# Filtered up and down sampling on half-array tiles, with the middle rows in passes of their own and one pinned order

## The chip, the cores and the metric

The kernel runs on one core of one Trainium2 chip. The metric is the device time in microseconds. The kernel before takes 1045.09 us, the median of three runs (1044.65, 1045.09 and 1049.59).

## The reference

The input `x` has the shape (4, 32, 128, 128): 4 batches, 32 tokens (channels) of 128 rows and 128 columns, in float32. Two layers follow each other, each a mixer and a recurrence, and each is added to its input:

```python
x = x + L0_conv(_ln_c(x), ...)          # attention over tokens with spectral convolutions
t = _to_tokens(x)                       # here 4 x 4096 x 128: tokens and rows in one axis
t = t + L0_ffn(_ln_t(t), W, V, ...)     # recurrence
x = _from_tokens(t, x)
x = x + L1_conv(_ln_c(x), bias, up_filter, dn_filter)
t = t + L1_ffn(_ln_t(t), W, V, ...)
```

`_ln_c` and `_ln_t` normalise each row of 128 numbers by its mean and variance. The recurrence multiplies the rows by W, normalises the products over all rows (batch norm), and then steps along the rows: `y = sigmoid(wx + y @ V.T)`.

The change is in the second layer's mixer, `L1_conv`:

```python
x = x + bias
x = x.reshape(B * C, 1, H, W)                       # 128 images of 128 x 128
x = jnp.repeat(jnp.repeat(x, 2, axis=2), 2, axis=3) # 256 x 256
x = _conv_same(x, up_filter)                        # 12 x 12, outer product of one 1-D filter
x = jax.nn.leaky_relu(x, negative_slope=0.2) * sqrt(2)
x = _conv_same(x, dn_filter)                        # 12 x 12, the same
x = x[:, :, ::2, ::2]                               # back to 128 x 128
```

Both filters are outer products, so each convolution is a product along the rows' axis and one along the columns' axis. Doubling and filtering along one axis is one matrix of 128 by 256, filtering and halving is one of 256 by 128. These matrices are banded: an output depends on a handful of neighbouring inputs only, since the filter has 12 taps at double resolution.

## The kernel before

The residual stays on the chip in `XA`, a tile of 128 partitions (the row h) by 4 batches, 32 tokens and 128 columns. `WXY` is one large tile that holds the recurrences' products and states; its last columns, `rest`, hold the convolution's matrices and starting states.

The function `parallel()` sets the stages. The first layer's mixer takes the time up to about 487 us; its instructions' order is written out by hand and pinned by `in_order()` (L433), which makes each instruction of PE, VectorE (DVE), ScalarE (ACT) and GpSimd (POOL) depend on the one before it on its engine. The first recurrence's scan (`scan()`, steps on L1846 to L1848) runs from 487 to about 548 us, in four segments side by side. Then comes the convolution stage (to about 961 us), then the second scan, which also adds the states to the residual and writes the output.

The convolution stage works on units of half a token, that is two images of 128 by 128; there are 64 units. Each unit passes through four functions:

- `up_rows` (L1976 to L1982): two products, each with an image of `XN` (128x128) as the stationary operand and the matrix `UR` of 256 columns as the moving one. The result lies transposed in PSUM. ACT copies its 512 columns to `q1` (L1981).
- `up_cols` (L1984 to L1993): for each half s of the 256 output positions, one product with `UC[s]` stationary and `q1` moving (512 columns); then leaky relu, as a relu on ACT (L1991) and a multiply and add on DVE (L1992), into `U`.
- `down_cols` (L1995 to L2004): eight products with a 128x128 piece of `U` stationary and `DC[s]` moving, two of them summed into each result; ACT copies to `q3` (L2003).
- `down_rows` (L2006 to L2012): two products with `DR[r]` stationary and 256 columns of `q3` moving, summed; DVE adds the result to `XA` (L2012).

Beside the units runs work on whole tokens or groups of up to four tokens. A table `beside` says at which step each is issued:

- `with_states`: the first recurrence's states of a token are turned (PE, L1900) and added to `XA` (DVE, L1931), and the rows' statistics are taken (L317).
- `input_norm`: scales and offsets of a group of tokens from these statistics. This is a chain of small DVE operations (L307 to L312), the addition of epsilon (DVE, L291), the power -1/2 (POOL, L292), the offset (DVE, L325) and the channel's bias (DVE, L1939).
- `input_images`: the scaled images `XN`, half of them on DVE (L1948), half on ACT (L1950).
- `complete`: statistics of the finished token and its store to DRAM (`turned`).
- `feature_norm`, `feature_rows`, `feature_columns`, `feature_products`: the norm, scaled rows (DVE L356, ACT L358), turned rows (PE L364, ACT L372) and products with W (PE L378, statistics on DVE L381, copy on ACT L385) for the second recurrence.

At step k the loop issues `down_rows(k-4)`, `down_cols(k-3)`, `up_cols(k-1)`, `up_rows(k)`, and then what `beside` lists. The stage isn't pinned: a scheduler orders the instructions by their dependencies. Groups are of 1, 1, 2 and then 4 tokens. `U` and `XN` have three buffers (pool `cv3`), the other tiles of the stage two. In PSUM, `ps_c1` has one buffer for each of five tags; turned rows use the two buffers of `ps_t`.

The eight filter matrices come by one DMA (L1907) ahead of the first scan.

## Time and profile before

| | us |
|---|---|
| median of three runs | 1045.09 |
| span of the profiled execution | 1043.7 |
| first scan's first product to its last (L1846) | 487.4 to 547.3 |
| convolution stage at its steady pace | 564 to 940 |
| last statistics of the second recurrence's products (L381) | 960.4 |
| mean granted TensorE clock over the span | 0.955 |

Busy time by stretch, in us:

| stretch | PE | DVE | ACT | POOL | granted clock |
|---|---|---|---|---|---|
| 0 to 360 (loads, mixer) | 305.8 | 271.5 | 224.5 | 69.1 | |
| 360 to 547.6 (mixer's end, first scan) | 164.6 | 166.8 | 158.6 | 55.1 | 0.99 |
| 547.6 to 564 (stage's start) | 12.2 | 13.8 | 4.7 | 2.0 | 0.69 |
| 564 to 940 (stage) | 370.6 | 235.8 | 211.0 | 43.9 | 1.00 |
| 940 to 961 (stage's end) | 17.4 | 13.6 | 14.0 | 2.0 | 1.00 |
| 961 to 1043.7 (second scan) | 69.2 | 72.3 | 52.5 | 0.6 | 0.90 |

PE, PEld, DVE, ACT, POOL and SP stand for TensorE's products, TensorE's weight loads, VectorE, ScalarE, GpSimd and SyncE. A group line of the profile gives the line of the code, the engine, the operation, the tiles (out<-in), for TensorE the tile of the array in use (128*128 is the whole of it, 64*128 is 64 rows by 128 columns), the shapes, and how many there were. The numbers after the bar are the busy time of the group in us, the mean of one in ns, and the idle time of the engine just before them with what ended most of it. A line of the timeline gives the start in us from the span's start and the length of a run of like instructions. A line of the stretches gives the busy time of each engine between two times, the granted clock, the share of the DMA engines and GB/s.

### The profile page before, as it was taken

The page shows a single profiled execution, that of the slowest core. Times are in us where ns is not written, and L with a number is a line of the kernel's source. Part 1 is how long each engine was busy: PE and PEld are TensorE (multiplying, and loading weights), DVE is VectorE, ACT ScalarE, POOL GpSimd, SP SyncE. Part 2 cuts the span into 40 slices and gives each one's busy share as a digit, 9 for nine tenths or more (in the row PEclk, how much of TensorE's full clock was granted, in tenths as well). Part 3 has the DMA queues.
Part 4 walks back from the last instruction along what each step waited for, and adds up shares of the span by engine and source line. Part 5 has one row for each costly group of instructions (what it writes and reads, how often), then busy time and mean ns, then how long its engine had stood idle before and what let it go on. Part 6 is the DMA issues. An engine that isn't in the chain of part 4 may idle for free.

```text
span 1043.7 us, 18129 instructions
## 1 busy us (share of the span) xinstructions
PE 939.8 (90%) x6422; PEld 679.4 (65%) x6422; DVE 773.7 (74%) x2501; ACT 665.3 (64%) x1606; POOL 172.8 (17%) x298
## 2 busy tenths in 40 slices
PE   3999899977888999877998999999999999998995
PEld 2565565775655555534776777777777777775884
DVE  5996487776688998988888565665666666466997
ACT  3756355766467999877883545464656555556874
POOL 1000000022444536441001111102020202100000
PEclk9999989977889999999998999999999999999998
DMA  9723000001011110200000001000000000004543
GB/s 235 175 36 76 1 1 1 1 1 42 21 42 41 42 42 22 82 21 1 1 1 1 21 21 31 21 21 21 22 21 21 21 21 28 24 21 166 212 163 131
DMA packets 68965, 48.83 MB, mean 47 GB/s; under 512 B 4417, under 2 KB 63809, under 8 KB 68801
## 3 DMA queue, kind: packets, MB, share of 16 engines
q1 hardware_dynamic: 68529, 47.31, 15.6%
q8 instruction: 53, 0.87, 0.4%
q0 software_dynamic: 288, 0.01, 0.2%
q10 hardware_dynamic: 48, 0.26, 0.1%
q14 instruction: 47, 0.39, 0.1%
HBM read 30.68 MB, written 16.88 MB: 46 GB/s over the span
## 4 chain that ended last, share of the span: by engine, by line
PE 47%; DVE 26%; ACT 8%; POOL 6%; issue 3%; POOLq 0%; DVEq 0%; ACTq 0%
PE ps_up L1989 8%; PE ps_scan L1846 7%; PE ps_dn L2001 6%; DVE XA L1516 4%; PE ps_up L1978 3%; DVE XA L1515 3%; PE ps_dn L2010 3%; PE ps_y L1235 2%; POOL c_r L292 2%; PE pm L987 2%; PE ps_wx L378 2%; DVE U L1992 2%; PE ps_inv L413 2%; DVE ps_scan L1847 2%; PE ps_st L1358 2%
## 5 line engine op out<-in xcount | busy, mean ns | idle before, releaser
L1992 DVE SCALAR_TENSOR_TENSOR U<-ps_up,above 128x512 f32<-128x512 f32 x128 | 86.7, 690 | 89.9 <-ACT above L1991 89.8
L1989 PE MATMUL ps_up<-q,WXY 128*128 128x512 f32 x256 | 124.0, 606 | 6.0 <-ACT q L1981 6.0
L2001 PEld LDWEIGHTS ps_dn<-WXY,U 128*128 128x128 f32 x1024 | 124.4, 192 | 3.3
L2001 PE MATMUL ps_dn<-WXY,U 128*128 128x128 f32 x1024 | 124.6, 275 | 0.0
L1847 DVE SCALAR_TENSOR_TENSOR ps_scan<-WXY,bs,ps_scan 128x128 f32<-128x128 f32 x352 | 101.7, 351 | 11.1 <-PE ps_scan L1846 9.7
L1991 ACT ACTIVATE above<-ps_up 128x512 f32<-128x512 f32 x128 | 74.4, 596 | 25.4 <-PE ps_up L1989 25.4
L2003 ACT COPY q<-ps_dn 128x512 f32<-128x512 f32 x64 | 37.5, 586 | 71.9 <-PE ps_dn L2001 71.9
L378 PE MATMUL ps_wx<-xt,wvt 128*128 128x512 f32 x128 | 68.0, 617 | 6.5 <-ACT WXY L385 4.5
L1978 PEld LDWEIGHTS ps_up<-WXY,XN 128*128 128x128 f32 x256 | 49.6, 194 | 34.8 <-issue 15.9
L292 POOL TENSOR_TENSOR f_r<-rs_e,neg_half 128x16 f32<-128x16 f32 (+2 forms) x10 | 24.0, 2396 | 278.4 <-DVE rs_e L291 278.4
L1989 PEld LDWEIGHTS ps_up<-q,WXY 128*128 128x128 f32 x256 | 44.0, 193 | 39.1 <-issue 23.9
L1978 PE MATMUL ps_up<-WXY,XN 128*128 128x256 f32 x256 | 67.4, 387 | 0.1
L2010 PE MATMUL ps_dn<-q,WXY 128*128 128x256 f32 x256 | 66.0, 380 | 0.0
L782 PE MATMUL ps_st<-cst,XA 128*128 128x130 f32 x256 | 43.7, 311 | 14.7 <-ACT XA L765 11.6
L2010 PEld LDWEIGHTS ps_dn<-q,WXY 128*128 128x128 f32 x256 | 46.1, 190 | 16.4 <-issue 12.0
L385 ACT COPY WXY<-ps_wx 128x512 f32<-128x512 f32 x60 | 35.0, 583 | 33.6 <-DVE bn L381 33.4
L1573 ACT ACTIVATE xn<-XA,f_o,f_r 128x128 f32<-128x128 f32 x120 | 50.9, 489 | 4.7 <-DVE f_o L1555 4.7
L782 PEld LDWEIGHTS ps_st<-cst,XA 128*128 128x128 f32 x256 | 35.4, 207 | 27.8 <-ACT XA L765 12.7
L1352 ACT ACTIVATE Z<-Z,k,aB 128x128 f32<-128x128 f32 x128 | 51.1, 481 | 3.5 <-DVE Z L1347 3.2
L1515 DVE SCALAR_TENSOR_TENSOR XA<-ps_inv,r1B,xin 128x128 f32<-128x128 f32 x128 | 44.1, 344 | 8.8 <-PE ps_inv L1508 8.8
L1516 DVE SCALAR_TENSOR_TENSOR XA<-Z,gB,XA 128x128 f32<-128x128 f32 x128 | 46.5, 363 | 5.0
L1950 ACT ACTIVATE XN<-XA,c_o,c_r 128x128 f32<-128x128 f32 x64 | 28.8, 490 | 31.5 <-DVE c_o L1939 25.5
(433 smaller groups left out, 2135.0 us busy)
## 6 DMA issues: line engine op xcount, KB each, us to landing
XA<-in_x_dram SPq DMA_DIRECT2D x16, 512.0 KB, 7.9
xin<-in_x_dram SPq DMA_DIRECT2D x32, 256.0 KB, 3.1
turned<-XA SPq DMA_DIRECT2D x32, 256.0 KB, 2.3
XA<-turned SPq DMA_DIRECT2D x8, 1024.0 KB, 14.6
out_dram<-res SPq DMA_DIRECT2D x64, 128.0 KB, 2.1
WXY<-dd SPq DMA_DIRECT2D x4, 544.0 KB, 10.6
WXY<-md SPq DMA_DIRECT2D x4, 144.0 KB, 4.9
WXY<-m1d SPq DMA_DIRECT2D x1, 544.0 KB, 10.9
```

Source lines behind the costliest of these rows:

```text
L378: mm(self.held[t], self.t[:, 0, :], xt, start=True, stop=True)
L782: mm(p[:, i, :], XA[:, b, t0 + j + i, :], cst[:, C_E : C_E + 130], start=True, stop=True)
L1515: stt(a, p2[c, b][:, i], r1B[:, j : j + 1], xin[c, b - b % 2][:, b % 2, i], ALU.mult, ALU.add)
L1516: stt(a, Z[c][:, b, i], gB[c][:, n : n + 1], a, ALU.mult, ALU.add)
L1846: mm(p4, self.t[:, 1, :], prev, start=True, stop=True)
L1847: stt(p4, WX[:, :, h, :], s[:, 0:1], p4, ALU.mult, ALU.add)
L1978: mm(p[:, b, :], XN[u // 2][:, (u % 2) * H2 + b, :], UR.rearrange("p r q -> p (r q)"), start=True, stop=True)
L1989: mm(p, UC[:, s, :], q, start=True, stop=True)
L1991: nc.scalar.activation(above, p, AF.Relu, scale=1.0 - SLOPE)
L1992: stt(U[:, s], p, SLOPE, above, ALU.mult, ALU.add)
L2001: mm(p[:, r, b, :], U[:, s, b, r * P : (r + 1) * P], DC[:, s, :], start=(s == 0), stop=(s == 1))
L2010: mm(p, DR[:, r, :], q[:, r], start=(r == 0), stop=(r == 1))
```

## The change

The banded matrices are cut, so that products run on half of the array's rows or half of its columns.

- The image's 128 rows and columns are cut into two halves of 64. `up_rows` multiplies, for each half of the image's rows, only with the 67 positions (`E`) of each phase that this half reaches, so that there are two products of 64 rows and 134 columns for each image, into two tiles `p1a` and `p1b`. Positions close to the cut need both halves.
- `up_cols` likewise has, for each of two parts and two halves, a product of 64 rows with 268 moving columns.
- Because `down_cols` for a half of the outputs needs rows beyond the cut, the middle rows get passes of their own: 16 columns around the cut of each of eight images (`XM`, copied by POOL) go through `up_rows` together as a third image in every fourth unit (so that they come out side by side on the 128 partitions), then through `mid_cols`, `mid_leaky`, `mid_down` and `mid_copy` (once for every eight images). `down_mid` (POOL) adds their contribution to the 12 middle columns of `q3`.
- `down_cols` has 16 products (32 MATMULs) for a unit, each on one half of the array's columns with 64 moving columns; `down_rows` has four products on column halves with 256 moving columns.
- Scalings move: of a token's four images three are scaled on POOL and one on ACT (`input_images`); of the feature rows two on POOL and two on ACT.
- The filters come in 32 small DMAs instead of one, after two memsets on POOL.
- The whole stage stands under `in_order()`. A step now issues the table `early`, then `down_mid(k-3)`, `up_cols(k-1)`, `up_rows(k)`, leaky relu and copies, `down_cols(k-2)`, `down_rows(k-3)`, and then the table `beside`. The statistics and norms, scalings, copies of turned rows and products' statistics stand in `early`; turned states, turned rows, products and the middles' products stand in `beside`. The recurrence's check stands in step 5 of `early`.
- Groups are of 2, 2 and then 4 tokens. `U` and `XN` have two buffers; an `XN` now holds eight images.

```diff
-        filt = rest[:, : 8 * P].rearrange("p (m n) -> p m n", m=8)
-        nc.sync.dma_start(filt, bass.AP(hankel.tensor, hankel.offset, [[1, P], [2 * P, 8], [1, P]]))
-        UR, UC, DR, DC = (filt[:, 2 * k : 2 * k + 2] for k in range(4))
+        filt = rest[:, : 4 * P].rearrange("p (m n) -> p m n", m=4)
+        UR, DR = filt[:, 0:2], filt[:, 2:4]
+        UC = rest[:, 4 * P : 5 * P]
+        DC = rest[:, 6 * P : 7 * P].rearrange("p (k n) -> p k n", k=2)
+        UCm = rest[:, 7 * P : 7 * P + 12 * NI]
+        DCm = rest[:, 12 * P : 12 * P + 12 * NI].rearrange("p (i n) -> p i n", i=NI)
+        nc.gpsimd.memset(rest[:, 6 * P : 8 * P], 0.0)
+        nc.gpsimd.memset(DCm, 0.0)
...
+            in_order(),
...
+            def input_middles(g):
+                XM[g] = cv.tile([P, NI, 16], F32, tag="XM", name="XM")
+                nc.gpsimd.tensor_copy(XM[g], XN[g][:, :, 56:72])
...
-                    if b % 2 == 0:
-                        ts(XN[t][:, b, :], XA[:, b, t, :], r(b), o(b), ALU.mult, ALU.add)
+                    dst, src_ = XN[t // 2][:, t % 2 * NB + b, :], XA[:, b, t, :]
+                    if b < 3:
+                        nc.gpsimd.tensor_scalar(dst, src_, r(b), o(b), ALU.mult, ALU.add)
...
             def up_rows(u):
...
+                n = H2 + (u % 4 == 0)
+                x_ = XN[u // 4]
+                p = [ps_c1.tile([P, H2 + 1, 2, E], F32, tag=f"p1{k}", name="ps_up1") for k in "ab"]
+                for i in range(n):
+                    for k in range(2):
+                        q = slice(HALF * k, HALF * k + HALF)
+                        a = XM[u // 4][q].rearrange("p i w -> p (i w)") if i == H2 else x_[q, u % 4 * H2 + i, :]
+                        mm(p[k][:, i], a, UR[q, :, P - E :] if k == 0 else UR[q, :, :E], start=True, stop=True)
...
+            def up_cols(u):
+                q = q1.pop(u)
+                pu[u] = [ps_c1.tile([P, H2, 2, P], F32, tag=f"u{k}", name="ps_up2") for k in range(2)]
+                for part in range(2):
+                    for k in range(2):
+                        h = slice(HALF * k, HALF * k + HALF)
+                        dst = pu[u][k][:, :, :, P - E :] if part == 0 else pu[u][k][:, :, :, :E]
+                        mm(dst, UC[h], q[part][h, :H2],
+                           start=(part == 0), stop=(part == 1), skip_group_check=True)
...
+            def mid_cols(g):
+                q = q1.pop(("mid", g))
+                p = pm_[g] = ps_t.tile([P, 2, P], F32, tag="t", name="ps_um")[: 12 * NI]
+                for part in range(2):
+                    mm(p[:, :, P - E :] if part == 0 else p[:, :, :E], UCm, q[part][:, H2],
+                       start=(part == 0), stop=(part == 1), skip_group_check=True)
...
             def down_cols(u):
...
+                            for c in range(2):
+                                o = slice(HALF * c, HALF * c + HALF)
+                                mm(p3[u][o, r, b, HALF * k : HALF * k + HALF], v[:, k, b, r, o], DC[:, k, :],
+                                   start=True, stop=True)
...
+            def down_mid(u):
+                i = u % 4 * H2
+                a = q3[u][:, :, :, 58:70]
+                nc.gpsimd.tensor_tensor(a, a, q3m[u // 4][:, :, i : i + H2, :], ALU.add)
...
+            for k in range(FIRST, max(early) + 1):
+                for f, args in early.pop(k, ()):
+                    f(*args)
                 if 0 <= k - 3 < units:
+                    down_mid(k - 3)
                 if 0 <= k - 1 < units:
+                    up_cols(k - 1)
+                if 0 <= k < units:
+                    up_rows(k)
+                if 0 <= k - 1 < units:
+                    up_cols_leaky(k - 1)
+                if 0 <= k < units:
+                    up_rows_copy(k)
+                if 0 <= k - 2 < units:
+                    down_cols(k - 2)
+                    down_cols_copy(k - 2)
+                if 0 <= k - 3 < units:
+                    down_rows(k - 3)
+                    down_rows_add(k - 3)
                 for f, args in beside.pop(k, ()):
                     f(*args)
+                    if f is mid_cols:
+                        mid_leaky(*args)
```

## The prediction

> **What bounds the kernel now.** I read the page's busy shares and costliest groups first, then the busy time by stretches, then one unit of the convolution stage in the timeline.

> ```profile
> PE 939.8 (90%) x6422; PEld 679.4 (65%) x6422; DVE 773.7 (74%) x2501; ACT 665.3 (64%) x1606; POOL 172.8 (17%) x298
> L1989 PE MATMUL ps_up<-q,WXY 128*128 128x512 f32 x256 | 124.0, 606 | 6.0 <-ACT q L1981 6.0
> L2001 PE MATMUL ps_dn<-WXY,U 128*128 128x128 f32 x1024 | 124.6, 275 | 0.0
> ```

> The convolutions' products are the costliest groups of TensorE (PE). Each product is issued as two MATMULs (1024 = 64 units x 8 x 2).

> ```profile
> 547.60:564.00 16.40, 12.22 (x42) 7.90 (x42) 13.76 (x60) 4.70 (x12) 2.03 (x2) 0.69 0.00 0
> 564.00:940.00 376.00, 370.63 (x1985) 283.95 (x1984) 235.76 (x738) 210.98 (x413) 43.90 (x16) 1.00 0.08 22
> 663.59:713.16 49.57, 49.22 (x265) 37.73 (x265) 31.89 (x100) 28.41 (x57) 5.80 (x2) 1.00 0.08 22
> ```

> Columns: stretch, length, busy PE, weight loads, VectorE (DVE), ScalarE (ACT), GpSimd (POOL), granted clock. From 564 to 940 us PE is busy for 370.6 of 376 us at full clock: it is the bound. The last row is one period of eight units, 49.6 us.

> ```profile
> 700.34 1.88 PE L1989 MATMUL ps_up<-q,WXY 128*128 128x512 f32 x4
> 702.05 1.03 PE L1978 MATMUL ps_up<-WXY,XN 128*128 128x256 f32 x4
> 702.92 1.02 PE L378 MATMUL ps_wx<-xt,wvt 128*128 128x512 f32 x2
> 703.78 1.03 PE L2010 MATMUL ps_dn<-q,WXY 128*128 128x256 f32 x4
> 704.64 1.95 PE L2001 MATMUL ps_dn<-WXY,U 128*128 128x128 f32 x16
> 706.42 0.59 PE L1989 MATMUL ps_up<-q,WXY 128*128 128x512 f32 x1
> ```

> Starts follow without holes: columns up 1.71, rows up 0.87, product 0.86, rows down 0.86, columns down 1.78, in all 6.08 us a unit; 512 columns take 0.428 us.

> ```profile
> 100.71 1.94 PE L802 MATMUL ps_pr<-A,cst 128*64 128x512 f32 x8
> 326.45 1.13 PE L428 MATMUL ps_inv<-invq,cst 64*128 64x512 f32 x4
> 69.56 1.26 PE L868 MATMUL pg<-WXY 128*64 128x64 f32 x18
> ```

> Other stages use half-array tiles already. Eight MATMULs of 512 columns on two column halves take 1.94 us (alone 3.4), four on two row halves 1.13 (alone 1.7): two run at once, in both shapes. Pieces of 64 moving columns on one column half (L868) follow each other in about 0.06 us.

> ```profile
> 623.44 0.69 DVE L1931 TENSOR_TENSOR XA<-XA,ps_y 128x512 f32<-128x512 f32 x1
> 626.20 0.16 DVE L291 TENSOR_SCALAR rs_e<-ln_v 128x16 f32<-128x16 f32 x1
> 626.53 2.90 POOL L292 TENSOR_TENSOR c_r<-rs_e,neg_half 128x16 f32<-128x16 f32 x1 [8.93 <-DVE rs_e L291]
> 629.46 0.17 DVE L325 SCALAR_TENSOR_TENSOR c_o<-ln_m,c_r 128x16 f32<-128x16 f32 x1 [3.10 <-POOL c_r L292]
> 629.67 0.62 DVE L1939 TENSOR_SCALAR c_o<-c_o,sc 128x4 f32<-128x4 f32 x4
> ```

> A norm of four tokens: from the states' addition to the shifted offset 6.85 us, of which POOL's power takes 2.90 while DVE waits. Twice in eight units this runs now, under a PE that stays busy: three buffers of U (two after the change) and queues in no pinned order cover it.

> [...] pairs overlap, and from 326.45 to the next full-array start at 327.51 pass 1.06 us for 0.86 us of streaming, 0.2 for the changes. [...] in the trace DVE sits 3.10 us before the offset. [...] Here the stretch 547.60 to 564, with PE's holes at its start, has a clock of 0.69.

> **The change, by parts.** Step k of the new loop issues up_cols(k-1), up_rows(k), down_cols(k-2), down_rows(k-3), then the work "beside".
> - up_cols: 2 x 2 MATMULs of 268 columns, pairs overlapping, 0.23 each: 0.91 (was 1.71).
> - up_rows: 2 images and a quarter of a third (the middles), 134 columns, 0.116 a pass: 0.52 (0.87).
> - down_cols: 32 MATMULs on column halves, 64 moving columns each, in 16 pairs of 0.06: 0.95 (1.78). No overlapping pair of this small shape is in the trace; between 0.93 and, not overlapping, 1.9. I take 0.95, because [...] 4-fold pairs of 128 columns overlap elsewhere.
> - down_rows: twice the instructions at half the width, 0.87, as before.
> - middles: (2 x 2 x 0.116 + 4 x 0.111)/4 = 0.23, new.
> - three changes of tile shape a step: 0.55, new.
> - turned rows, products and states: 0.87, unchanged. The recurrence's check, moved from the stage's start to step 5, stays on DVE (about 2 us) and fits there.
> Sum 4.9 a step against 6.08; by k modulo 4 it is 4.4, 5.5, 4.6, 5.0, or 39.1 for eight. If PE stayed the bound, 64 x 1.19 = 76 us would go.

> The other engines have room in sum. ACT: 2 x 0.6 leaky, 2 x 0.4 copies of 268, 0.59, about 1.5 for norms' images, turned rows and copies: 4.1 a step. DVE 3.6, relieved of both scalings. POOL takes 20 scalings in eight steps; a 128x128 one with pointers isn't in the trace: POOL's 128x128 TENSOR_TENSOR takes 0.49, its 128x896 TENSOR_SCALAR 2.48, so 0.45 to 0.9; I take 0.6, some 2.6 us a step with the powers. Sums don't bind; order does, for every queue is now pinned.

> *Feature norm step (k = 11, 19, ... 51, 59).* down_mid(k-3) is queued on POOL behind that step's power, and PE's down_rows waits for it. From the step's start: DVE ends the addition at 0.3, statistics 1.2, seven chained small operations 2.45, power 2.5 to 5.4, middles' copy and down_mid 6.1. PE would be there at 2.5; down_rows starts at 6.2, and states and product behind it: 8.75 for 5.05, **+3.7**.

> *Input norm step (k = 12, 20, ... 52), the next one.* DVE's queue: states' addition, statistics, small operations, wait for the power, offset and bias (6.75 after the states are in PSUM), only then the products' statistics (0.7). ACT's queue: the copy of the product (waits for those, 0.6), two feature rows (0.9), and only then the two leaky passes (1.1) and the copies q1 that PE needs next; DVE's last leaky pass frees the bank 10.9 us after the states' end, 9.9 after the step's start, for 4.5: **+5.4**.

> *Steps k = 2 modulo 4.* The same chain without norm, behind the middles' leaky pass: 5.85 for 4.6, **+1.25** twice. k = 0: +0.4.

> So eight steps take 39.1 + 3.7 + 5.4 + 2.5 + 0.4 = 51.1 us against 49.6.

> *The whole stage*, by starts of up_cols. Unit 0: 561.2 for 557.5, since two tokens' norms and six POOL scalings stand before it, with the clock at half. Unit 11: steps 1 to 11 have no feature work, 4.0 to 4.8 each, plus waits at 4 and 11: 617 for 620.1. Unit 51: five periods, 872.6 for 867.7. Step 52: 9.9; steps 53 to 63 carry no states, 58.7 with waits at 59 and 63: unit 63 at 941 for 939.4. Tail: last norm over two tokens, their rows one after the other on ACT: 23 to the last statistics for 21. In sum +4 us.

> *Filters.* 32 small DMAs replace one on SP's queue; at 0.42 us an issue they run from about 419 to 437 between the xin loads at 423.7 and 440.6, so they cost nothing; without that gap, up to 10 us. POOL's two memsets (0.4) fall into its gap at 422 to 425. The order of PE, DVE and ACT before the stage is the same.

> *Clock.* [...] about 3.1 for each of six pairs of norm steps, 19 us. Bounds: 0, and 6 for each pair and 3 for each single one, 45.

> Sum against the profiled execution: span 1043.7, +4, +19, and 1.4 around it (median 1045.09; runs 1044.65 to 1049.59): **1068 us**.

> **Rivals.**
> 1. Same waits, full clock: 1049 (1040 to 1057). For it: between 564 and 940 holes of up to 1.4 us kept 1.00. Against: the holes are three times that.
> 2. PE keeps the bound: faster. Place: the norm steps; if power and statistics run under the preceding step, so that both steps together lose 3.5 instead of 9.1, a period is 45.5 us, and 1049 - 5.6 x 5 is about 1021 (968 if all is hidden). It decides below 49.6 a period, some 1.5 us less waiting than I count. For it: the same norms cost PE 0.4 us a period now. Against: down_mid and q1 stand behind them in pinned queues.
> 3. Half tiles don't overlap: PE 8.1 a step, 8 x (6.08 - 8.1) lost a period, about 1170. Against: both shapes overlap above.

> **How the numbers follow.** Waits and half clock 0.54, rival 1 0.24, rival 2 0.13, rival 3 0.04, clock lost over most of the stage (above 1096) 0.05. Likeliest 1068, its own range 1052 to 1096; with rival 1 and the slow edge of rival 2: 1036 to 1096. A measurement tells about 0.5% (5.2 us) from no change. Faster: rival 2 and a little of 1, 0.14. Same: most of rival 1, 0.18. Slower 0.68.

> **What would show it.** Right: up_cols' starts 51 to 56 us apart over eight units; PE under 85% busy there, with granted clock under 1; DVE idle 3 us before f_o and c_o; down_rows waiting for POOL's q3, up_cols for DVE or ACT; down_cols' 32 MATMULs within 1.0 to 1.2 us. Wrong: periods below 48; clock 1.00 throughout (rival 1); down_cols near 2 us (rival 3); POOL scalings over 1 us, which would move all steps.

## The result

The changed kernel takes 1069.99 us (median of four runs, 1069.37 to 1070.86), the kernel before 1044.87 us beside it. The ratio is 1.0241, with a 95% interval of 1.0209 to 1.0272: slower. The profiled execution has a span of 1067.6 us against 1043.7 us, 23.9 us more.

The page of the changed kernel, its busy shares and the groups that answer to those shown of before:

```profile
PE 902.9 (85%) x8406; PEld 641.3 (60%) x8406; DVE 747.9 (70%) x2373; ACT 659.4 (62%) x1670; POOL 262.3 (25%) x538
L386 ACT COPY WXY<-ps_wx 128x512 f32<-128x512 f32 x60 | 34.9, 582 | 116.9 <-DVE bn L382 116.9
L2049 PE MATMUL ps_up<-q,WXY 64*128 64x268 f32 x512 | 91.1, 461 | 7.4 <-ACT q L2038 5.0
L2111 PE MATMUL ps_dn<-q,WXY 128*64 128x256 f32 x512 | 67.0, 383 | 32.9 <-POOL q L2103 32.9
L2093 PE MATMUL ps_dn<-WXY,U 128*64 128x64 f32 x2048 | 83.3, 242 | 0.0
```

PE has 37 us less work than before (939.8) although it has more instructions and part of it ran at half clock (granted clock 0.89 from 564 to 940 us, below). It is no longer busy for 99% of the stage. Two waits stand out: `down_rows` waited 32.9 us for the middles' addition on POOL, and ACT's copy of the product waited 116.9 us for DVE's statistics (33.4 before).

The busy time by stretches, with the columns as in the prediction:

```profile
547.00:564.00 17.00, 9.02 (x62) 7.21 (x61) 11.86 (x53) 4.41 (x12) 6.79 (x11) 0.80 0.00 0
564.00:940.00 376.00, 318.90 (x3694) 238.31 (x3696) 205.53 (x605) 195.69 (x450) 119.73 (x226) 0.89 0.07 21
648.50:703.10 54.60, 46.04 (x513) 34.21 (x512) 29.08 (x87) 27.78 (x65) 17.09 (x32) 0.87 0.07 20
```

A period of eight units takes 54.6 us instead of 49.6, with PE busy for 84% of it at a granted clock of 0.87. DVE, ACT and POOL are each busy for little more than half of the period or less. So no engine is the bound; waits are.

The two norm steps, in the timeline (in brackets: the idle time of the engine before a line, and what ended it). The feature norm step begins with `up_cols` (L2049) at 770.09 us, ahead of these lines, the input norm step with the one at 777.49:

```profile
771.53 2.91 POOL L293 TENSOR_TENSOR f_r<-rs_e,neg_half 128x16 f32<-128x16 f32 x1 [8.38 <-DVE rs_e L292]
774.64 0.27 POOL L2103 TENSOR_TENSOR q<-q,q3m 128x48 f32<-128x48 f32 x1
774.97 1.08 PE L2111 MATMUL ps_dn<-q,WXY 128*64 128x256 f32 x8 [0.92 <-POOL q L2103]
776.73 0.69 DVE L1954 TENSOR_TENSOR XA<-XA,ps_y 128x512 f32<-128x512 f32 x1 [0.21 <-PE ps_y L1901]
777.49 1.17 PE L2049 MATMUL ps_up<-q,WXY 64*128 64x268 f32 x8
779.27 1.15 PE L2093 MATMUL ps_dn<-WXY,U 128*64 128x64 f32 x32
779.65 2.91 POOL L293 TENSOR_TENSOR c_r<-rs_e,neg_half 128x16 f32<-128x16 f32 x1 [4.74 <-DVE rs_e L292]
782.60 0.17 DVE L326 SCALAR_TENSOR_TENSOR c_o<-ln_m,c_r 128x16 f32<-128x16 f32 x1 [3.02 <-POOL c_r L293]
783.62 0.68 DVE L382 BATCH_NORM_STATS2 bn<-ps_wx 128x6 f32<-128x512 f32 x1
783.73 1.08 PE L2111 MATMUL ps_dn<-q,WXY 128*64 128x256 f32 x8 [3.31 <-POOL q L2103]
784.34 0.58 ACT L386 COPY WXY<-ps_wx 128x512 f32<-128x512 f32 x1 [9.61 <-DVE bn L382]
785.60 1.07 ACT L2055 ACTIVATE above<-ps_up 128x512 f32<-128x512 f32 x2
786.56 0.90 ACT L2038 COPY q<-ps_up 128x402 f32<-128x402 f32 x2
787.11 2.16 PE L2049 MATMUL ps_up<-q,WXY 64*128 64x268 f32 x7 [0.88 <-ACT q L2038]
```

Read it from the end. `up_cols` at 787.11 waits for ACT's copies q1 (786.56). These stand behind the leaky passes, those behind scaled rows and the copy of the product, which waited 9.61 us for DVE's statistics (783.62), which stood behind the norm, which waited 3.02 us for POOL's power. From 777.49 to 787.11 is one step: 9.62 us, where the same step takes 4.32 us when PE waits for nothing (in the ordered kernel below). The halved tiles work as costed: the 32 MATMULs of `down_cols` take 1.15 us (full clock), and eight of `up_cols` 1.17 from the first start to the last end.

### The profile page after: what moved, and what is told of

The parts are those of the page before. It is cut to its first block, busy times and chain, and to the rows that moved or that the text cites. A ratio compares the mean times of both kernels' runs of the same rounds, so it can differ in the third digit from the quotient of the medians.

```text
span 1067.6 us, 22407 instructions
## 1 busy us (share of the span) xinstructions
PE 902.9 (85%) x8406; PEld 641.3 (60%) x8406; DVE 747.9 (70%) x2373; ACT 659.4 (62%) x1670; POOL 262.3 (25%) x538
## 3 DMA queue, kind: packets, MB, share of 16 engines
q8 instruction: 68, 1.11, 0.4%
## 4 chain that ended last, share of the span: by engine, by line
PE 41%; DVE 21%; issue 13%; POOL 8%; ACT 6%; DVEq 0%; ACTq 0%; POOLq 0%
PE ps_scan L1847 5%; PE ps_up L2049 5%; PE ps_dn L2093 4%; DVE XA L1517 4%; PE ps_dn L2111 3%; DVE XA L1516 3%; PE ps_up L2030 3%; PE ps_y L1236 2%; POOL c_r L293 2%; POOL f_r L293 2%; PE ps_wx L379 2%; PE pm L988 2%; PE ps_inv L414 2%; PE ps_st L1359 2%; DVE bn L382 2%
## 5 line engine op out<-in xcount | busy, mean ns | idle before, releaser
L1848 DVE SCALAR_TENSOR_TENSOR ps_scan<-WXY,bs,ps_scan 128x128 f32<-128x128 f32 x352 | 101.2, 350 | 10.7 <-PE ps_scan L1847 9.6
L386 ACT COPY WXY<-ps_wx 128x512 f32<-128x512 f32 x60 | 34.9, 582 | 116.9 <-DVE bn L382 116.9
L2049 PE MATMUL ps_up<-q,WXY 64*128 64x268 f32 x512 | 91.1, 461 | 7.4 <-ACT q L2038 5.0
L2111 PE MATMUL ps_dn<-q,WXY 128*64 128x256 f32 x512 | 67.0, 383 | 32.9 <-POOL q L2103 32.9
L2093 PE MATMUL ps_dn<-WXY,U 128*64 128x64 f32 x2048 | 83.3, 242 | 0.0
L2093 PEld LDWEIGHTS ps_dn<-WXY,U 128*64 128x64 f32 x2048 | 74.2, 154 | 10.3 <-ACT above L2055 3.8
L2049 PEld LDWEIGHTS ps_up<-q,WXY 64*128 64x128 f32 x512 | 53.8, 207 | 32.2 <-issue 16.8
L2111 PEld LDWEIGHTS ps_dn<-q,WXY 128*64 128x64 f32 x512 | 31.2, 137 | 45.3 <-POOL q L2103 35.3
L2030 PEld LDWEIGHTS ps_up<-WXY,XN 64*128 64x128 f32 x512 | 52.5, 224 | 5.5 <-issue 0.3
L365 PE MATMUL ps_xt<-ident,xn 128*128 128x128 f32 x256 | 48.1, 304 | 9.1 <-ACT xt L373 2.8
L382 DVE BATCH_NORM_STATS2 bn<-ps_wx 128x6 f32<-128x512 f32 x64 | 43.7, 687 | 14.4 <-PE ps_wx L379 14.4
L2030 PE MATMUL ps_up<-WXY,XN 64*128 64x134 f32 x512 | 53.5, 316 | 0.0
```

Source lines behind the costliest of these rows:

```text
L365: nc.tensor.transpose(p[:, b, :], xn[:, b, :], ident)
L382: nc.vector.bn_stats(self.stats[:, t, :], self.held[t].rearrange("p b w -> p (b w)"))
L1848: stt(p4, WX[:, :, h, :], s[:, 0:1], p4, ALU.mult, ALU.add)
L2030: mm(p[k][:, i], a, UR[q, :, P - E :] if k == 0 else UR[q, :, :E], start=True, stop=True)
L2049: mm(dst, UC[h], q[part][h, :H2], start=(part == 0), stop=(part == 1), skip_group_check=True)
L2093: mm(p3[u][o, r, b, HALF * k : HALF * k + HALF], v[:, k, b, r, o], DC[:, k, :], start=True, stop=True)
```

## The experiments

The theory: the saved PE work is real, but in the pinned queues the waits of the norms (and what is queued behind them) take more than was saved, and the clock is halved behind the holes (0.87 in the period above, 1.00 in that of before). The rivals: POOL's order alone is at fault; the small MATMULs are; half clock falls only where PE waits anyway. A step is counted from one unit's `up_cols` to the next; steps 33 to 40 (from unit 32) are one period, 35 the feature norm step, 36 the input norm step.

**The middles' addition ahead of the power.** POOL's order in the norm steps, nothing else (with the copy `mid_copy` that the addition needs):

```diff
+                first = any(f in norms for f, _ in work) and 0 <= k - 3 < units
+                if first:
+                    ...                      # mid_copy, then
+                    down_mid(k - 3)
                 for f, args in work:
                     f(*args)
-                if 0 <= k - 3 < units:
+                if 0 <= k - 3 < units and not first:
                     down_mid(k - 3)
```

> Only POOL's order changes: in the norm steps the addition of the middles (and the copy it needs) goes ahead of the power. Theory of the prediction (each norm step has its own chain: POOL's queue in the feature norm step, DVE's and ACT's queues in the input norm step): only the wait of 1.1 us in the feature norm step goes, with about 1 us that the half clock adds there; in the input norm step up_cols still waits for q1 behind the norm, so it stays near 9.6 us. Six periods of about 2 us: 1058 us (1052 to 1066). Rival (POOL's order alone sets both norm steps): 1.1 + 3.3 us go from each period, with the half clock 6 us: 1034 to 1046. Rival (the waits are cover for TensorE work that is as long): 1070.

Measured: 1066.31 us, ratio to before 1.0215 (1.019 to 1.024). That is just over the upper end of my own range, and not far below the 1070 of the last rival. POOL's order alone, as the cause of both norm steps, is ruled out. In the profiled execution step 35 fell from 7.40 to 6.58 us and step 36 grew from 9.62 to 10.69, so that the period stayed at 54.6 us. The timeline of the changed order shows why the gain was handed on:

```profile
772.83 0.48 DVE L326 SCALAR_TENSOR_TENSOR f_o<-ln_m,f_r 128x16 f32<-128x16 f32 x1 [3.58 <-POOL f_r L293]
773.23 1.28 DVE L2056 SCALAR_TENSOR_TENSOR U<-ps_up,above 128x512 f32<-128x512 f32 x2
774.31 1.19 PE L2049 MATMUL ps_up<-q,WXY 64*128 64x268 f32 x7
774.76 0.68 DVE L1954 TENSOR_TENSOR XA<-XA,ps_y 128x512 f32<-128x512 f32 x1
785.00 2.16 PE L2049 MATMUL ps_up<-q,WXY 64*128 64x268 f32 x7 [0.88 <-ACT q L2038]
```

PE has no hole left in step 35: the same work takes 5.01 us at full clock (in the ordered kernel below), and the rest of the 6.58 us is half clock (`up_rows` and the 32 MATMULs of `down_cols` take 1.11 and 1.92 us, where full clock gives 0.62 and 1.15), which in the changed kernel passed under the wait for POOL (clock 0.77 in its step 35). PE starts step 36 earlier (774.31), but DVE has the feature norm's wait (3.58 us) ahead of its leaky passes and adds the states only at 774.76, 0.45 us after the step's start instead of 0.76 before it. The input norm's chain begins with that addition, and from there to the next `up_cols` it takes as long as before (10.2 us, 10.4 in the changed kernel). So the two norm steps are one chain over DVE's queue, and what step 35 gives up, step 36 takes. In step 59, which no input norm follows, the gain stays (6.09 us instead of 7.90).

**Statistics and copy of the product ahead of the norm, too.** In the norm steps `feature_copy` (DVE and ACT) is issued before the norm.

> As the kernel with the middles' addition first; in the norm steps the product's statistics (DVE) and copy (ACT) go ahead of the norm too. Theory (POOL's queue and the DVE and ACT chain stand side by side in the input norm step, so that taking one away gives nothing): ACT has q1 early, and the bank is freed by DVE's last leaky pass after the norm, at about 7.5 us: the step goes from 10.7 to 7.5 to 8 us, with the half clock behind it about 4 us a period: 1038 to 1048 us. Rival (the norm's wait on DVE alone sets the step): 9.5 or more, 1058 to 1068.

Measured: 1053.65 us, ratio 1.0103 (1.0071 to 1.0136). ACT now has q1 in time, and step 36 falls from 10.7 to 8.3 to 8.9 us, which is less than expected and outside both figures. What is left of the step in its trace: PE's turned rows wait 3.2 us for POOL's scalings behind the power, and DVE's leaky passes end 9.1 us after the step's start, since my 7.5 us had left out that the states' addition now comes after it.

**Each norm cut in two.** Statistics and power stay; offset and bias go to the next step's `early`:

```diff
-                r, o = affine(stats.pop(("c_st", t0)), n, 1e-6, "c")
+                half["c", t0] = affine_a(stats.pop(("c_st", t0)), n, 1e-6, "c")
+
+            def input_offset(t0, n):
+                r, o = affine_b(*half.pop(("c", t0)))
...
                 at(early, last, input_norm, t0, n)
+                at(early, last + 1, input_offset, t0, n)
```

and the same for the feature norm. Both were cut in one kernel, and each alone in two more (all with the middles' addition first).

> As the kernel with the middles' addition first, and each norm is cut in two: statistics and power in one step, offset and bias in the next step's early table, so that neither DVE nor POOL is waited for within a step. Theory (the waits behind the norms in pinned queues take all that the half tiles save, and open the holes that halve the clock): a period falls from 54.7 us to 43 to 47 us, since step contents of 39 us and the waits of the other steps (k = 2 modulo 4) are left: 1005 to 1030 us. Rival (half tiles themselves are the cost: many small MATMULs and shape changes): 1060 or more. Rival (another pinned chain takes the place, ACT's scalings and copies): 48 to 52 us a period, 1035 to 1058.

> As the kernel with the middles' addition first, and only the feature norm is cut in two; the input norm is whole. Theory (after the first runs: the two norm steps are one chain over DVE, two powers behind each other in its queue, and what a step gives up the next one takes until DVE waits once less): DVE's leaky passes and additions of the feature norm step come some 1 us sooner, and the input norm step starts its own chain that much earlier: about 1 to 1.5 us a period, 1057 to 1062 us. Rival (the feature norm step has its own cost of 2.4 us, of which taking POOL's queue out gave 0.8): 2 to 4 us a period, 1042 to 1054.

> The same with only the input norm cut in two; the feature norm is whole. Theory: the input norm's wait on DVE is the long one, since products' statistics, ACT's copy, leaky and q1 stand behind it: its step falls from 10.7 to 6 or 7 us, with less half clock behind it, 4 to 6 us a period: 1032 to 1044 us. Rival (the feature norm's wait lets the next step start late anyway): 1050 or more.

Measured: both 1025.48 us (ratio 0.9821, 0.9797 to 0.9845), within the theory's range, although a period (46.8 to 48.4 us) lies at or just above the upper end of the 43 to 47 us expected; the feature norm alone 1053.78 (1.0093, 1.0072 to 1.0115), the input norm alone 1045.47 (1.0001, 0.9981 to 1.0021). Against the 1066.31 us of the kernel with the middles first that is 12.5 us for the feature norm, 20.8 for the input norm and 40.8 for both, more than their sum. The feature norm alone missed my range to the better and lies just within that of the rival: step 36 fell to 9.3 us as expected, but step 35 also took 5.0 us instead of 6.6 in every other period. The input norm alone missed its range by 1.5 us: step 36 is 7.4 to 8.0 us, since the feature norm still delays DVE ahead of it and POOL's scalings stand behind the power. With both cut, steps of 6.5 us remain: those with k = 2 modulo 4, the half clock behind them (granted clock 0.93 from 691.6 to 739.9 us), and the input norm step itself.

**The stage unpinned.** `in_order()` is taken out of the changed stage.

> The changed stage without the pinned order, the scheduler orders its queues; passes, tiles and buffers as in the changed kernel. Theory (pinning exposes the norms): waits mostly go, a period of 42 to 48 us, 1005 to 1040 us. Rival (two buffers of U and XN, and POOL as a link of the chain, hold it whatever the order): within 1 percent of the changed kernel, 1060 to 1080.

Measured: 1020.93 us, ratio 0.9771 (0.9747 to 0.9794), as the theory had it; between units 16 and 48 a period takes 45.6 to 48.4 us. With the same passes, tiles, buffers and POOL scalings the changed kernel is faster than the one before. So buffers and small MATMULs aren't what cost.

**The pin alone.** The kernel before, with `in_order()` put on its convolution stage:

```diff
             tc.tile_pool(name="ps_c1", bufs=1, space=PSUM) as ps_c1,
+            in_order(),
         ):
```

> The kernel before, whole tiles and its own order of issue, with its convolution stage pinned: the pin alone. Theory (pinning exposes the norms whatever the tiles): the two norm steps of a period lose 3 to 6 us together, less than in the changed kernel, since leaky stands ahead of the norms in its step: 1060 to 1085 us. Rival (the pin costs only because the half tiles leave less TensorE work to cover with): 1044 to 1052.

Measured: 1077.6 us, ratio 1.0325 (1.0304 to 1.0346). A period takes 52.0 to 53.7 us between units 16 and 56 instead of 48.8 to 49.7. One of its steps takes 9.2 to 10.8 us instead of 6.2, and none of the others is longer by more than 0.1 us. The timeline of that step:

```profile
796.01 0.18 DVE L325 SCALAR_TENSOR_TENSOR c_o<-ln_m,c_r 128x16 f32<-128x16 f32 x1 [3.10 <-POOL c_r L292]
796.75 0.69 DVE L381 BATCH_NORM_STATS2 bn<-ps_wx 128x6 f32<-128x512 f32 x1
797.48 0.58 ACT L385 COPY WXY<-ps_wx 128x512 f32<-128x512 f32 x1 [6.69 <-DVE bn L381]
797.75 0.33 PE L364 MATMUL ps_xt<-ident,xn 128*128 128x128 f32 x1 [1.61 <-DVE xn L356]
```

The same chain shows: offset after the power, then the statistics, then ACT. Of the 27.5 us by which this profiled execution is longer than that of the kernel before, 15.7 fall between units 16 and 56; the rest lies before and after these units and was not looked into. The pin costs 34 us on whole tiles and 49 us on half tiles (1069.99 against 1020.93). All the rest of the change gains 24 us unpinned and 8 us pinned; its parts (half tiles, scalings on POOL, order of issue, fewer buffers) were not measured one by one.

**The holes filled.** Idle products, ident by 110 columns of ident, fill PE's holes; their results are not used. With them the granted clock was 1.00 in a period of the second version below, against 0.87 in the changed kernel. The first version wrote them to spare columns of the tiles of `up_rows`.

> The changed kernel with idle products of 110 columns (results unused, in spare columns of the banks of up_rows) filled into TensorE's holes of the norm steps and ahead of the middles' second products. Waits stay, the holes don't. Theory (half clock adds to the waits): the clock is 1.00 from unit 12 to unit 52, a period of 50 to 51.5 us, and the time 1043 to 1052 us. Rival (half clock falls only where TensorE waits anyway): 1066 to 1075, clock near 1.00 all the same.

It measured 1104.7 us, ratio 1.0573 (1.0546 to 1.06), and told nothing on the question, because the filling itself waited:

```profile
800.95 6.52 PE L2024 MATMUL ps_up<-ident 128*128 128x110 f32 x30 [6.68 <-ACT q L2046]
```

The idle products write to a tile that ACT had yet to copy, although to other columns of it; with the wait of 6.68 us and their own 6.52 us (0.21 us from one start to the next, where eight later ones have 0.11) step 36 took 18.55 us instead of 9.62. Steps 37 and 39, which in the changed kernel have a clock of 0.71 and 0.74, fell from 7.82 and 6.60 us to 5.47 and 5.01. The second version puts them right ahead of `down_rows`, into the unused half of its own tile:

```diff
-                p4[u] = ps_t.tile([P, H2, P], F32, tag="t", name="ps_dn2")
+                whole = ps_t.tile([P, 4 * P], F32, tag="t", name="ps_dn2")
+                p4[u] = whole[:, : 2 * P].rearrange("p (b w) -> p b w", b=H2)
+                for _ in range(...):         # 8 or 15, by the step
+                    mm(whole[:, 2 * P : 2 * P + 110], ident, ident[:, :110], start=True, stop=True)
```

> As the first filling, in which the idle products waited for ACT's copies of the bank that they wrote, which lengthened the input norm step to 18.6 us. Now they are issued right ahead of down_rows into the other half of its own PSUM tile: 8 in steps k = 2 modulo 4 and in the feature norm step, 15 in the input norm step, fewer microseconds than TensorE waits there. Theory (half clock adds 3 to 4 us a period to waits that stay): clock 1.00 in the period, 50 to 51.5 us a period, 1043 to 1052 us. Rival (half clock falls only where TensorE waits anyway): 54 to 55 us a period, 1066 to 1074.

Measured: 1061.47 us, ratio 1.0163 (1.0145 to 1.0182). In its undisturbed periods:

```profile
808.30:860.00 51.70, 50.38 (x591) 39.13 (x590) 29.22 (x87) 27.72 (x65) 17.09 (x32) 1.00 0.08 22
```

The clock is 1.00 and the period 51.8 us from one `up_cols` to the eighth after it; the filling itself lengthens steps 34 and 38 by 0.32 us each, so the waits alone come to 51.1, and half clock to 3.5 us a period (54.6 less 51.1). The whole came out above my figure: a period gained 2.8 us and not 3.5, one of them (53.3 us, clock 0.97) kept a stretch of half clock, and between units 8 and 16, where steps have fewer holes, the filling cost 2.0 us. The rival that half clock costs nothing is ruled out by the period.

**Every queue in an order of its own making.** Both norms cut; within a step first the offsets, the middles' addition and the scalings, then statistics and norms (so that POOL's power comes last), then the passes with leaky and q1, and only then the product's statistics and copy:

```diff
+                rank = (mid_copy, feature_offset, input_offset, None, feature_columns, feature_rows, input_images,
+                        input_middles, group_stats, complete, f0.check, feature_norm, input_norm, feature_copy)
...
+                issue(rank[:3])
+                if 0 <= k - 3 < units:
+                    down_mid(k - 3)
+                issue(rank[4:13])
...
                     down_cols_copy(k - 2)
+                issue(rank[13:])
```

> As the kernel with norms cut in two, and within a step: offsets first, the middles' addition, scalings, then statistics and norms (POOL's power last), and the product's statistics and copy behind the leaky passes and q1. Theory (the order within pinned queues is all that keeps TensorE from being the bound): no step over 6 us, a period of 40 to 44 us, clock 1.00: 975 to 1000 us. Rival (ACT, with some 4.2 us of work a step, or the round trip from up_cols over leaky to q1, sets a floor): 45 to 48 us a period, 1005 to 1025.

Measured: 979.25 us, ratio 0.9375 (0.9357 to 0.9393). A period and its input norm step (unit 35's `up_cols` at 736.50):

```profile
721.00:760.70 39.70, 39.19 (x515) 29.05 (x514) 28.83 (x87) 27.59 (x64) 17.13 (x32) 1.00 0.10 28
```

```profile
739.27 2.91 POOL L293 TENSOR_TENSOR c_r<-rs_e,neg_half 128x16 f32<-128x16 f32 x1 [1.14 <-DVE rs_e L292]
740.30 0.69 DVE L382 BATCH_NORM_STATS2 bn<-ps_wx 128x6 f32<-128x512 f32 x1
740.82 1.17 PE L2068 MATMUL ps_up<-q,WXY 64*128 64x268 f32 x8
742.22 0.24 DVE L1969 SCALAR_TENSOR_TENSOR c_o<-c_m,c_r 128x16 f32<-128x16 f32 x1 [0.91 <-POOL c_r L293]
```

PE is busy for 99% of the period at full clock: it is the bound again, at 39.7 us for eight units instead of 49.6. The power runs past the step's end, under PE's next unit, and DVE waits 0.91 us for it, with nothing urgent behind it. Products, tiles and the division of work among the engines are those of the changed kernel; only the order of issue differs (and each norm keeps its means in a tile of its own), which is worth 90.7 us (1069.99 against 979.25).

**The check later.** In that kernel `f0.check`, with which DVE compares the ends of the first scan's segments, goes from the head of step 5 to the end of step 8.

> As the ordered kernel; the first recurrence's check goes from the head of step 5, where it holds DVE 2.6 us ahead of the leaky passes, to the end of step 8. TensorE has a hole of 3.7 us behind it in step 5 and half clock after that: 4 to 6 us less, 973 to 976 us. Rival (step 5 waits for the norm of the first full group anyway): 978 to 980.

Measured: 973.29 us, ratio 0.9318 (0.9299 to 0.9336). The step from unit 4 to unit 5 fell from 9.47 to 6.10 us and the next from 6.28 to 4.12. This is the fastest kernel of the study, 6.8% below the kernel before.

## Why the prediction was right

The sum gave 1068 us; 1069.99 was measured, and the span moved by 23.9 us where 23 were forecast. The cause was named rightly: the norms' waits in pinned queues, and the half clock behind PE's holes. That the number came within 2 us is in part luck, because terms were off both ways:

| us | forecast | measured |
|---|---|---|
| PE work of eight units | 39.1 | 39.7 (period of the ordered kernel) |
| feature norm step 35 | 8.75 | 7.40 |
| input norm step 36 | 9.9 | 9.62 |
| steps 34 and 38 | 5.85 each | 6.51 each |
| waits and work of a period | 51.1 | 51.1 (filled, less the filling) |
| half clock in a period | 3.1 | 3.5 |
| up_cols of unit 0 | 561.2 | 560.0 |
| up_cols of unit 0 to that of unit 11 | 55.8 | 58.5 |
| of unit 11 to unit 51, with the half clock | 271 | 268.2 |
| last up_cols to the last statistics' end | 23 | 26.7 |

- *PE work.* The costs read from other stages' half tiles held. In the ordered kernel the next group starts 0.99 us after `down_cols` and 1.00 us after `up_cols`, where 0.95 and 0.91 were said. Rival 3 is out.
- *Input norm step.* Right in place and size: DVE 3.02 us ahead of the offset, then statistics, copy, rows, leaky, q1. PE also waited 3.31 us there for POOL's addition behind the power, but under this chain: with the addition first the step was no shorter.
- *Feature norm step.* Right in kind, too large: `down_mid` behind the power was put down at 3.7 us and cost 2.4 (7.40 us less the 5.01 of work). The power was to begin 2.5 us into the step and began 1.44 us in (771.53 less 770.09), because DVE ran ahead of PE and ended the statistics at 770.20. What the prediction missed is that the two norm steps are one chain: taking `down_mid` out of POOL's way saved 0.8 us here, and the next step took it back. That the wait for POOL sets this step shows in the filled kernel, where it is still 7.40 us at full clock and `down_rows` still starts 4.88 us after `up_cols`, as in the changed kernel:

```profile
820.93 1.17 PE L2049 MATMUL ps_up<-q,WXY 64*128 64x268 f32 x8
825.81 1.08 PE L2116 MATMUL ps_dn<-q,WXY 128*64 128x256 f32 x8 [0.20 <-POOL q L2103]
```

- *Steps 34 and 38.* The period's sum came out because these are 0.66 us longer each than forecast: 5.04 us of work (ordered kernel) where 4.6 was said, and 1.47 of waiting, for the tile of the middles' second products, where 1.25 was said.
- *Half clock.* Right that half clock follows holes; the size is near (3.1 and 3.5 us a period), the places are not. The 3.1 us for a pair of norm steps and the bounds around it were my estimate, which no trace of before gave, and I put it behind both norm steps. Behind the feature norm step none follows, and the half clock within it costs nothing (7.40 us with and without). It falls behind the input norm step (step 37: clock 0.71, 7.82 us, 5.92 in the filled kernel) and behind the 1.7 us hole of step 38 (step 39: clock 0.74, 6.60 us for 5.01).
- *Start and tail.* The clock was at half ahead of unit 0, as said: 0.50 from 554 to 557 us, in both kernels. Units 0 to 11 took 2.7 us more than forecast and the tail 3.7 us more; what made the tail longer was not tried.
- *The check.* "Fits there" was wrong at least where PE is the bound: moving it is worth 6.0 us in the ordered kernel. What it cost in the changed kernel itself was not tried.
- *Filters.* Right: their DMAs are issued from 421.7 to 436.5 us, and the first scan starts at 487.0 us (487.4 before). A 128x128 scaling on POOL takes 0.44 us, the low end of my bounds (0.45), not 0.6.
- *Rival 2* (PE keeps the bound) is what the ordered kernel does: I had put it at 968 us if all is hidden, and 973.29 was reached. It needed another order, not another change of tiles.

Rival 1 (same waits, full clock, 1049 us) is out by the clock of 0.87 in the period. What the filled kernel would measure without any half clock or wasted filling was not run; its 3.5 us a period are worked out from its periods.

## What to carry to other kernels

When a change takes work from the bounding engine, write down for one period what each pinned queue has standing behind its longest wait; if engine sums leave room, the place of a few small instructions decides (here it was worth 90.7 us). A chain with a long foreign operation in it (here the power on POOL) should be issued in two parts, with its second part behind a whole step of other work (here 40.8 us for both norms). And measure a pin and a new tiling apart: here one cost 34 to 49 us and hid the gain of the other.
